# A scan pipeline in which the gated convolution starts two steps later on even steps, and 73 products change their engine

## The chip, the cores and the metric

The kernel runs on one core of a Trainium2 chip. Its time is the device time of one execution in microseconds (us); three executions before the change took 28298.65 us in the median (28296.38 to 28321.09). One further execution was recorded by the profiler; every duration below comes from that one.

## The reference

Two layers work on 8 images of 64 channels and 128 x 128 pixels, in float32. The first is a filter whose 3 x 3 weights are computed for each pixel (a convolution, a softmax over nine taps, a weighted sum of shifted pixels). The second is longer. Cut to what matters:

```
x_norm = ln4d(input)                       # layer norm over channels
seq = layernorm(x_norm as 16384 tokens)
for i in range(2):                         # two blocks, each scanned in both directions
    x, z = in_proj(rmsnorm(seq))
    yf = mamba_dir(x, z, forward);  yb = flip(mamba_dir(flip(x), flip(z), backward))
    seq = seq + out_proj(yf + yb)
x4 = conv3x3(rmsnorm(seq)) + residual
x = input + depthwise3x3(conv1x1(x_norm)) * x4
g1, g2 = split(depthwise3x3(conv1x1(ln4d(x))))      # 170 channels each
return x + conv1x1(gelu(g1) * g2)

# mamba_dir, for 128 channels d and 16 states n, along the tokens:
h = exp(softplus(dt) * A) * h + dt * B * u          # the recurrence
y = (sum over n of h * C + D * u) * silu(z)
```

The recurrence is the bulk: 8 images x 2 blocks x 2 directions x 128 channels x 16 states, each over 16384 tokens.

## The kernel before

**Chunks and steps.** A chunk is 1024 tokens of one image, block and direction. There are 512 of them, 64 to an image, and chunk i starts at step 16 i. A step `t` is one scan over 128 rows (32 channels times 4 states) of the chunk, so there are 8192 steps, 1024 to an image; `u` is the number of the step in its chunk, 0 to 15. "Step 9 of a chunk" below means u = 9. The chunk's work is in `Chunk.plan`:

- `drive` (L1236): GpSimd multiplies dt*u by B for two scans at once, 128 x 2048, into `bu` (4 buffers), on odd steps, five steps ahead of its first scan.
- `decay` (L1244): ScalarE's exponential for one scan, into one of two PSUM buffers `w`, two steps ahead.
- `scan` (L1263 one way, L1265 the other): VectorE's recurrence over 1024 tokens. It writes back to `w`, or to `hs` in SBUF where the product will be made on GpSimd.
- `product` (L1280 on VectorE, L1282 and L1284 on GpSimd): h times C. `on_pool(u)` chooses: odd u and u = 4, 12 go to VectorE in the same step, the other even u to GpSimd a step later, six in a chunk. An even step that follows a gelu (`gelu_times`) has its product on VectorE too.
- `keep` (L1287): ScalarE copies the last column as the next chunk's state. A column and the two buffers `w` tie ScalarE's exponentials to the product of two steps before.
- `collect` (L1295, L1302): TensorE sums the states of a pair of scans into `y`, at steps 4, 5, 7, 9, 12, 13, 15 and 17 of the chunk. `y` is one PSUM buffer, two halves of the chunk take it in turn; `y_out` empties it at steps 11 and 3 (L1317 on VectorE in a direction's second pass, where it also applies the gate; L1319 on ScalarE in the first pass).

The inputs of chunk i + 2 are made beside it, through one PSUM buffer `mm`: `xp` (L1111) is issued at steps 6 and 7, the gate's `zp` (L1126) at 8 and 9, `dp` (L1153) at 13 and 14, `bcp` (L1172) at 15. ScalarE empties each a step later (L1117, L1134, L1160, L1179), applies silu at step 11 (L1137, L1139) and softplus at step 2 (L1166), each between two loads of an activation table. The output projection `op` (L1331, L1334) is issued at step 4, also through `mm`, and emptied by L1337 and L1344 at step 6.

**Three more stages run beside the scans**, each over 16 row groups of an image: the front (filter and first norms of the next image, from step 593 of an image, 24 steps a group), the mix (both 3 x 3 convolutions, the product, a norm, from step 990, 13 steps a group, so it ends in the next image's step 200), and the FFN (the gated convolution of the image before, from step 1202, that is step 178 of the next image, 24 steps a group). So in images 1 to 6 the mix lies beside steps 990 to about 180, the FFN beside 178 to about 562, the front beside 569 to about 993. The last image has no front beside it: its steps from about 562 to 826 have the scans alone, and its mix starts at 826.

The FFN of a group at step a: windows are loaded; three groups of `conv` (L932, L938) are issued in four parts each, at a to a+3, a+6 to a+9 and a+14 to a+17; they write the PSUM buffers `acc` and `bg`. ScalarE copies the first group's result (`first_out`, L980, a+5) and applies `gelus` (L987, L989, a+11, between two table loads). VectorE multiplies: `rest_times` (L994) at a+13, `times` (L997) for half 0 at a+19 and half 1 at a+21. `project` (L1012 to L1018) follows at a+21, ScalarE empties it (`add`, L1024) at a+23. 24 is one and a half chunks, so two successive groups begin at u = 2 and u = 10; 48 steps, two groups and three chunks make one period.

The front's softmax for a group: less_max and exps on VectorE and ScalarE, `sums` on VectorE (L588), `softmax` on GpSimd (L592), then three `piece` copies on ScalarE (L596) with two `less_piece` subtractions on GpSimd (L600) between them, then `turn` on TensorE (L605) and `turned` on ScalarE (L609).

**Order.** Nothing is scheduled by a tool. Every piece is put under a key (step, phase) and the program is issued in the order of the keys; inside a step the phases are FEED, SCAN, MID, PROD, EXP, DECAY, REST. An engine works its instructions strictly in that order, so a late one holds up all that stand behind it. SyncE issues the loads and stores, in the same order.

Of the kernel before, what the change touches and what calls it, by code (L numbers as in the profile page):

```python
# [21 lines left out]
NCH = HALF // ROWS  # L22
# [9 lines left out]
NT = 2 * NCH * N // T  # L32
# [4 lines left out]
FEED, SCAN, MID, PROD, EXP, DECAY, REST = range(7)  # L37

IMAGE = 4 * NT * U
FRONT_STEP, MIX_STEP, FFN_STEP = 24, 13, 24  # L40
FRONT_AT, MIX_AT, FFN_AT = 593, 990, 1202

SILU, SOFTPLUS, GELU = 11, 18, 11

# [11 lines left out]
def kernel(ctx: ExitStack, tc: tile.TileContext, a: dict, out: bass.AP):  # L56
# [131 lines left out]
    with tc.tile_pool(name="wspill", bufs=1) as fp, tc.tile_pool(name="wprep", bufs=2) as pp, \  # L188
            tc.tile_pool(name="wps", bufs=4, space=PSUM) as pps:
        with tc.manual_schedule():  # L190
# [104 lines left out]
            for k in range(9):  # L295
                i, j = divmod(k, 3)
# [28 lines left out]
            for q, ((g, c0, r0, n), fn, fdn) in enumerate(parts):  # L325
# [7 lines left out]
                for k in range(9):  # L333
                    i, j = divmod(k, 3)
# [26 lines left out]
            for l in range(DEPTH):  # L361
# [3 lines left out]
                for d in range(2):  # L365
# [5 lines left out]
                    now, i = taps, 2 * l + d + 1  # L371
                    if i < 2 * DEPTH:
                        taps = by_taps(inx2[i // 2], dirs[i][0], DI, KC)
                    for j in range(KC):
                        t = turned(now[:, j, :], ident, P, DI)
                        at = j if d == 0 else KC - 1 - j
# [40 lines left out]
    def at(time, phase, fn, *args):  # L417
        steps.setdefault((time, phase), []).append((fn, args))
# [123 lines left out]
    class Front:  # L542
        def __init__(self, b, c):
            self.b, self.c, self.p = b, c, b % 2
            self.n1, self.n2, self.n3 = Norm(), Norm(), Norm()
            self.t, self.wbk, self.alone = {}, {}, False
# [149 lines left out]
        def plan(self, a):  # L696
            n1, n2, n3 = self.n1, self.n2, self.n3
            b = a - FRONT_STEP
            at(b - 5, REST, self.load_xa)
            for i in range(3):  # L700
                at(b + 1 + i, REST, self.hidden, i)
            at(b + 5, DECAY, self.hidden_out)
            at(b + 21, REST, self.logits)
            at(b + 23, DECAY, self.less_max)
            at(b + 23, DECAY, self.exps)
            at(b + 25, MID, self.sums)
            at(b + 25, REST, self.softmax)
            for i in range(3):
                at(b + 26 + 2 * i, DECAY, self.piece, i)
                if i < 2:  # L710
                    at(b + 27 + 2 * i, REST, self.less_piece, i)
            at(b + 31, REST, self.turn)
            at(b + 32, DECAY, self.turned)
            at(a + 6, REST, self.load_xb)
            for k in range(9):

                t = a + k
                at(t + 11, DECAY, self.weight, k)
                at(t + 12, MID, self.weighted, k)
                at(t + 13, REST, self.gather, k)  # L720
            at(a + 23, DECAY, self.filtered)
            at(a + 23, REST, self.store_x1)
            at(a + 23, REST, self.centered, acc_tile, "x1")
            at(a + 24, DECAY, self.centered_out)
            at(a + 25, REST, lambda: n1.means(bg_tile, self.sq))
            at(a + 26, DECAY, n1.means_out)
            at(a + 27, REST, n1.spread, bg_tile)
            at(a + 29, MID, self.scaled, n1)
            at(a + 29, DECAY, self.first_norm)
            at(a + 30, REST, self.pointwise)  # L730
            at(a + 31, DECAY, self.pointwise_out)
            at(a + 31, REST, self.store_rows, dw_img[self.p], "dwt")
            at(a + 31, REST, self.centered, acc_tile, "xn")
            at(a + 32, DECAY, self.centered_out)
            at(a + 33, REST, lambda: n2.means(acc_tile, self.sq))
            at(a + 34, DECAY, n2.means_out)
            at(a + 35, REST, n2.spread, acc_tile)
            at(a + 37, MID, self.scaled, n2)
            at(a + 37, DECAY, self.second_norm)
            at(a + 37, REST, self.store_h)  # L740
            late, end = (a + 46, a + 55) if self.c < NCH - 1 else (a + 37, a + 43)
            at(late, DECAY, self.third_square)
            at(late + 1, REST, lambda: n3.means(bg_tile, self.sq))
            at(late + 2, DECAY, n3.means_out)
            at(end - 2, REST, n3.spread, bg_tile)
            at(end, MID, self.third_norm)
            at(end, REST, self.store_hn)
# [145 lines left out]
    class Ffn:  # L893
# [139 lines left out]
        def plan(self, a):  # L1033
            early = 12 if self.alone else 0
            at(a - 4 - early, REST, self.load, 0)
            at(a - 3 - early, REST, self.load, 1)

            if self.alone:
                at(a - 6, REST, self.before_taps)
                at(a - 5, DECAY, self.before_taps_out)  # L1040
                at(a - 5, REST, self.taps, 0)
                at(a - 2, REST, self.taps, 1)
                groups = ((0, 0, self.first_out, 2), (3, 1, self.times, 6))
                gelus, out = 3, 9
            else:
                groups = ((0, 0, self.first_out, 5), (6, 2, None, 0), (14, 1, self.times, 19))
                gelus, out = GELU, 21
            for t, g, end, to in groups:
                for i in range(4):
                    at(a + t + (0 if self.alone else i), REST, self.conv, g, i)  # L1050
                for h in range(2 if end else 0):
                    late = 0 if self.alone or end == self.first_out else 2 * h
                    at(a + to + late, MID if end == self.times else DECAY, end, h)
            at(a + gelus, REST, self.gelus)
            at(a + gelus + 2, MID, self.rest_times)
            at(a + out - 5, REST, self.load_x2)
            at(a + out, REST, self.project)
            at(a + out + 2, DECAY, self.add)
            at(a + out + 2, REST, self.store)
# [18 lines left out]
    class Chunk:  # L1078


        def __init__(self, i):
            self.b, self.l, self.d, self.t, self.second = order[i]
            self.i, self.t0 = i, U * i
            self.first = i % NT == 0
            self.pairs = PAIRS[i % 2]
            r, last = self.t0 % IMAGE, self.b == B - 1
            self.beside_front = (
                FRONT_AT - FRONT_STEP <= r < FRONT_AT + NCH * FRONT_STEP + 16 and not last
            ) or self.t0 < FIRST_FRONT_AT + (NCH - ALONE) * FRONT_STEP + 16
            self.prev = None  # L1090
            self.bus, self.hss, self.hs, self.ws = {}, {}, {}, {}
            self.dup, self.dtp, self.bp, self.cp, self.yv = {}, {}, {}, {}, {}
            self.norm = Norm()
# [128 lines left out]
        def on_pool(self, u):  # L1222


            if u % 2 or u % 8 == 4 or self.t0 + u - 1 in gelu_times:
                return False
            return True

# [221 lines left out]
    for b in range(B):  # L1450
        a, last = IMAGE * b, b == B - 1
# [36 lines left out]
```

## Time and profile before

| | us |
|---|---|
| median of three executions | 28298.65 |
| profiled execution | 28309.23 |
| its span, first to last instruction | 28307.4 |
| VectorE (DVE) busy | 26958.6 (95%) |
| GpSimd (POOL) busy | 26592.1 (94%) |
| TensorE (PE) busy | 23060.5 (81%) |
| ScalarE (ACT) busy | 18801.5 (66%) |
| one scan, L1263 or L1265 | 2.34 |
| one product on VectorE, L1280 | 1.22 |
| one product on GpSimd, L1282 / L1284 | 2.37 / 2.38 |
| one drive on GpSimd, L1236 | 4.55 |
| one decay on ScalarE, L1244 | 1.12 |

The page shows VectorE at "6999...97" tenths and GpSimd at "5999...94" over 40 slices: both are busy nearly always, in every slice but the first and the last. There are 5232 products on VectorE and 2960 on GpSimd, 8192 together. A busy share is an average over stages with different limits, so the useful views are the same ones over one stage: the busy times of a stretch (the windows view), who waited for whom in it (the waits view, which gives total, times and longest), and the instructions in order of time (the timeline).

### The profile page before, as it was taken

What the parts mean: (1) busy time and instruction counts of PE and PEld (TensorE: products, weight loads), DVE (VectorE), ACT (ScalarE), POOL (GpSimd) and SP (SyncE); (2) the same over time, 40 slices, a digit from 0 to 9 for tenths busy, and PEclk for the clock granted to TensorE, in tenths of its full rate; (3) what the DMA queues carried; (4) which work ended last, traced back from release to release, by engine and by line L of the source; (5) the groups of instructions that cost most, each with busy time, mean ns of one, the idle gap of its engine ahead of it and who ended that gap; (6) DMA issues with size and microseconds to landing.
All of it is one profiled execution on the core that took longest, in us unless ns stands there. A gap on an engine that the chain in (4) does not pass through costs nothing. (4 is left out here: it accounts for less than half of the span.)

```text
span 28307.4 us, 311814 instructions
## 1 busy us (share of the span) xinstructions
PE 23060.5 (81%) x98278; PEld 7346.2 (26%) x98278; DVE 26958.6 (95%) x17398; ACT 18801.5 (66%) x29144; POOL 26592.1 (94%) x7980
## 2 busy tenths in 40 slices
PE   8667888878888788888888888787888978888679
PEld 3212322223222232222322222222222222222113
DVE  6999999999999999999999999999999999999997
ACT  4666666666666666666666666666666666666663
POOL 5999999999999999999999999999999999999994
PEclk8778889988999889988889888998888988889789
DMA  6777787767877778777787777777777777777675
GB/s 178 233 239 229 238 262 247 249 227 239 267 243 248 230 240 266 247 242 231 246 257 249 242 232 246 259 249 237 233 253 251 252 234 238 251 251 249 217 251 153
DMA packets 2611073, 6796.34 MB, mean 240 GB/s; under 512 B 433558, under 2 KB 739110, under 8 KB 2608390
## 3 DMA queue, kind: packets, MB, share of 16 engines
q1 hardware_dynamic: 2608534, 6776.25, 73.7%
q8 instruction: 776, 12.71, 0.2%
q14 instruction: 883, 7.23, 0.1%
q10 hardware_dynamic: 880, 0.14, 0.0%
HBM read 5543.05 MB, written 1265.19 MB: 241 GB/s over the span
## 5 line engine op out<-in xcount | busy, mean ns | idle before, releaser
L1236 POOL TENSOR_TENSOR bu<-dup,bp 128x2048 f32<-128x2048 f32 x4096 | 18600.2, 4549 | 59.5 <-DMA bp<-bc_dram 23.8
L1244 ACT ACTIVATE w<-dtp,a_neg 128x1024 f32<-128x1024 f32 x8192 | 9163.6, 1119 | 1444.9 <-DVE hs L1265 586.8
L1280 DVE TENSOR_TENSOR hs<-w,cp 128x1024 f32<-128x1024 f32 x5232 | 6390.3, 1221 | 191.1 <-DMA cp<-bc_dram 41.0
L1265 DVE TENSOR_TENSOR_SCAN w<-w,state,bu 128x1024 f32<-128x1024 f32 x2651 | 6210.2, 2343 | 90.7 <-ACT w L1244 60.3
L1263 DVE TENSOR_TENSOR_SCAN w<-w,state,bu 128x1024 f32<-128x1024 f32 x2581 | 6048.3, 2343 | 124.7 <-ACT w L1244 105.3
L1302 PE MATMUL y<-hs,sel_y 128*32 128x512 f32 x32768 | 4953.0, 682 | 580.9 <-POOL hs L1284 449.1
L1287 ACT COPY state<-w 128x1 f32<-128x1 f32 x5232 | 828.5, 158 | 5159.7 <-DVE hs L1280 5100.4
L1282 POOL TENSOR_TENSOR hs<-hs,cp 128x1024 f32<-128x1024 f32 x1515 | 3590.8, 2370 | 507.5 <-DVE hs L1263 316.3
L1284 POOL TENSOR_TENSOR hs<-hs,cp 128x1024 f32<-128x1024 f32 x1445 | 3432.9, 2376 | 394.0 <-DVE hs L1265 366.1
L1263 DVE TENSOR_TENSOR_SCAN hs<-w,state,bu 128x1024 f32<-128x1024 f32 x1515 | 3550.5, 2344 | 159.4 <-ACT state L1287 79.9
L1265 DVE TENSOR_TENSOR_SCAN hs<-w,state,bu 128x1024 f32<-128x1024 f32 x1445 | 3384.4, 2342 | 76.8 <-ACT state L1287 43.3
L1111 PE MATMUL xp<-hn,wx 128*128 128x512 f32 x4096 | 2502.6, 742 | 1171.9 <-ACT xc L1117 561.7
L932 PE MATMUL fp<-fw,bgw 128*128 128x512 f32 (+1 forms) x5760 | 2123.0, 614 | 37.8 <-DMA fw<-xn_dram 34.5
L1153 PE MATMUL dp<-xc,wdt 128*128 128x512 f32 x2048 | 1328.2, 735 | 690.6 <-ACT dt L1160 390.3
L1302 PEld LDWEIGHTS y<-hs,sel_y 128*32 128x32 f32 x32768 | 719.7, 114 | 4287.9 <-issue 2594.1
L1295 PE MATMUL y<-xc,dskip 128*64 128x512 f32 x4096 | 1371.0, 754 | 417.8 <-ACT yv L1319 315.5
L1111 PEld LDWEIGHTS xp<-hn,wx 128*128 128x128 f32 x4096 | 849.0, 225 | 2656.4 <-issue 1047.3
L68 ACT ACT_TABLE_LOAD x1137 | 1458.8, 1283 | 20.9 <-PEq L1477 0.7
L1117 ACT ACTIVATE xc<-xp,cbias 128x512 f32<-128x512 f32 x1024 | 701.7, 685 | 1151.4 <-PE xp L1111 1149.1
L938 PE MATMUL fp<-fw,bgw 64*128 64x512 f32 (+1 forms) x5760 | 1379.1, 605 | 0.0
L634 PE MATMUL acc<-t,ident 128*128 128x512 f32 x2250 | 1353.6, 690 | 0.0
L619 PE MATMUL wb<-wt,sel_k 65*128 65x512 bf16 x1152 | 509.4, 443 | 992.9 <-DVE t L623 988.5
(220 smaller groups left out, 26201.6 us busy)
## 6 DMA issues: line engine op xcount, KB each, us to landing
bp<-bc_dram SPq DMA_DIRECT2D x4096, 256.0 KB
dup<-du_dram SPq DMA_DIRECT2D x4096, 256.0 KB
dtp<-dt_dram SPq DMA_DIRECT2D x4096, 256.0 KB
cp<-bc_dram SPq DMA_DIRECT2D x4096, 256.0 KB
hn<-hn_dram SPq DMA_DIRECT2D x1024, 256.5 KB
dt_dram<-dt SPq DMA_DIRECT2D x512, 512.0 KB
du_dram<-du SPq DMA_DIRECT2D x512, 512.0 KB
yf_dram<-yv SPq DMA_DIRECT2D x512, 256.0 KB
```

Source lines behind the costliest of these rows:

```text
L68: nc.scalar.preload_act_table_set("natural_log_exp_and_others")
L932: nc.tensor.matmul(o, wpair[:, i, g, m], self.win[h][:, i : i + ROWS, 0:W], start=(i == 0), stop=False)
L938: nc.tensor.matmul(o, wlast[rows, i, g, m], self.win[h][rows, i : i + ROWS, lo : W + lo], start=False, stop=(i == 2),)
L1111: nc.tensor.matmul(self.xp[h], wx[:, self.l, self.d, i, :], self.hn2[:, s.start + 2 * i : s.stop + 2 * i], start=(i == 0), stop=(i == 1),)
L1236: nc.gpsimd.tensor_tensor(bu, self.dup[self.pairs[k][1]], self.over_pair("bp", k), ALU.mult)
L1244: nc.scalar.activation(w, self.dtp[gp][:, i, :], AF.Exp, scale=a_neg[:, self.l, self.d, g, j : j + 1])
L1263: nc.vector.tensor_tensor_scan(to, w, bu, s0, ALU.mult, ALU.add)
L1265: nc.vector.tensor_tensor_scan(to[:, ::-1], w[:, ::-1], bu[:, ::-1], s0, ALU.mult, ALU.add)
L1280: nc.vector.tensor_tensor(out, hs, c, ALU.mult)
L1282: nc.gpsimd.tensor_tensor(out, hs, c, ALU.mult)
L1284: nc.gpsimd.tensor_tensor(out[:, ::-1], hs[:, ::-1], c[:, ::-1], ALU.mult)
L1302: nc.tensor.matmul(self.y[lo : lo + 32, :], sel_y, hs[:, i, s], start=False, stop=(k % 4 == 3))
```

## The change

The FFN starts at step 1204 in place of 1202, and its VectorE products move to even steps: `rest_times` from a+13 to a+14, both `times` to a+20 (from a+19 and a+21). `project` moves from a+21 to a+20, `load_x2` and `add` with it. As the gelus stand at a+11, the even step whose product goes to VectorE because of them moves from u = 14 and 6 to u = 0 and 8. The front's `softmax`, its pieces, `turn` and `turned` move one step back. Last, in every second chunk that has neither front nor FFN beside it, from chunk 16 on, the product of u = 8 goes to VectorE.

```diff
-FRONT_AT, MIX_AT, FFN_AT = 593, 990, 1202
+FRONT_AT, MIX_AT, FFN_AT = 593, 990, 1204
...
-            at(b + 25, REST, self.softmax)
+            at(b + 26, REST, self.softmax)
             for i in range(3):
-                at(b + 26 + 2 * i, DECAY, self.piece, i)
+                at(b + 27 + 2 * i, DECAY, self.piece, i)
                 if i < 2:
-                    at(b + 27 + 2 * i, REST, self.less_piece, i)
-            at(b + 31, REST, self.turn)
-            at(b + 32, DECAY, self.turned)
+                    at(b + 28 + 2 * i, REST, self.less_piece, i)
+            at(b + 32, REST, self.turn)
+            at(b + 33, DECAY, self.turned)
...
-                groups = ((0, 0, self.first_out, 5), (6, 2, None, 0), (14, 1, self.times, 19))
-                gelus, out = GELU, 21
+                groups = ((0, 0, self.first_out, 5), (6, 2, None, 0), (14, 1, self.times, 20))
+                gelus, out = GELU, 20
...
-                    late = 0 if self.alone or end == self.first_out else 2 * h
-                    at(a + to + late, MID if end == self.times else DECAY, end, h)
+                    at(a + to, MID if end == self.times else DECAY, end, h)
             at(a + gelus, REST, self.gelus)
-            at(a + gelus + 2, MID, self.rest_times)
+            at(a + gelus + (2 if self.alone else 3), MID, self.rest_times)
...
+            beside_ffn = FFN_AT - IMAGE <= r < FFN_AT - IMAGE + NCH * FFN_STEP and self.b
+            self.few_steps = self.i >= NT and not self.beside_front and not beside_ffn
...
             if u % 2 or u % 8 == 4 or self.t0 + u - 1 in gelu_times:
                 return False
+            if u == 8 and self.i % 2 and self.few_steps:
+                return False
             return True
```

Counted in the changed program, VectorE has 5305 products and GpSimd 2887: 73 have moved. By the conditions they lie in 10 chunks of image 0 (17 to 35), in 7 chunks of each of the seven mix stretches between images (49), in 7 chunks of the last image's scans alone, and in 7 beside its mix. The last image's own FFN, with nothing beside it, is as before.

## The prediction

> **What bounds the kernel now.** The page puts VectorE at 95% and GpSimd at 94%, and the chain of work that ended last is followed there through too small a share of the span to choose. I therefore read, stage by stage, first the busy times of one stretch, then who waited for whom in it, then the timeline. The four stretches are the scans beside the mix, beside the FFN, beside the front, and alone (last image). The columns are start and end, length, then busy time and instructions by engine, TensorE's granted clock, DMA share, GB/s.
>
> ```profile
> 7193.70:7879.80 686.10, 553.71 (x2446) 157.54 (x2444) 652.71 (x379) 455.33 (x692) 678.59 (x195) 0.90 0.83 264
> 7879.80:9100.80 1221.00, 1063.47 (x4346) 324.90 (x4350) 1182.83 (x712) 839.86 (x1235) 1162.07 (x330) 0.94 0.74 244
> 9254.80:10648.00 1393.20, 1152.00 (x5201) 405.95 (x5200) 1350.52 (x945) 954.91 (x1561) 1324.68 (x423) 0.87 0.73 237
> 26520.00:27039.00 519.00, 280.78 (x894) 52.63 (x896) 485.74 (x260) 317.56 (x454) 519.00 (x151) 0.62 0.60 205
> ```
>
> The order of engines is PE, PEld, DVE, ACT, POOL. Scans alone: GpSimd is busy 519.00 of 519.00 us. FFN and front: VectorE is the busier one (97%). Mix: GpSimd has 99%, VectorE 95%. Whether GpSimd sets the pace there is told by VectorE's waits. Scans alone (window 26520 to 27039):
>
> ```profile
> DVE hs L1265 <- POOL bu L1236: 18.6, 29, 1.0
> DVE w L1265 <- POOL bu L1236: 7.5, 8, 0.9
> ```
>
> VectorE waits here for GpSimd's drive about four times a chunk. Mix (7193.7 to 7879.8):
>
> ```profile
> DVE hc L654 <- PE rb L514: 10.8, 5, 3.8
> DVE w L1263 <- ACT w L1244: 7.7, 7, 2.3
> DVE hs L1263 <- ACT w L1244: 4.7, 3, 2.7
> ```
>
> These are its three longest; no row of this view names a drive. GpSimd is just full there, and VectorE waits for TensorE and ScalarE. Beside the FFN (7879.8 to 9100.8), the same three engines:
>
> ```profile
> DVE yv L1317 <- PE y L1302: 7.8, 8, 2.6
> DVE w L1265 <- ACT w L1244: 6.1, 6, 1.7
> DVE ga L997 <- PE fp L938: 3.8, 4, 1.0
> DVE w L1263 <- ACT w L1244: 3.0, 2, 2.5
> ```
>
> The timeline tells why, first TensorE, then VectorE, at the second group of a period (xp is issued at u = 6, the group's last convolutions at u = 8 to 11):
>
> ```profile
> 8276.04 3.54 PE L1111 MATMUL xp<-hn,wx 128*128 128x512 f32 x4 [3.73 <-ACT state L1287]
> 8280.59 1.98 PE L1111 MATMUL xp<-hn,wx 128*128 128x512 f32 x4
> 8284.35 1.99 PE L932 MATMUL fp<-fw,bgw 128*128 128x512 f32 x4
> ```
>
> ```profile
> 8284.53 2.36 DVE L1265 TENSOR_TENSOR_SCAN w<-w,state,bu 128x1024 f32<-128x1024 f32 x1 [0.78 <-ACT w L1244]
> 8287.40 0.69 DVE L1317 TENSOR_TENSOR yv<-y,gate 128x512 f32<-128x512 f32 x1 [0.52 <-DMA o<-branch_dram]
> 8295.96 0.69 DVE L997 TENSOR_TENSOR ga<-ga,fp 128x512 f32<-128x512 f32 x1 [0.95 <-PE fp L938]
> ```
>
> TensorE idles 3.73 us before xp, then needs 3.54 us for four matmuls that take 1.98 us a little later. ScalarE's copy of xp is late, its exponentials behind it are late, and the convolutions stand in front of the collect that y_out needs.
>
> **The change, part by part.** All sums are against the profiled execution, 28309.2 us, which is 10.6 us above the median of the runs.
>
> *Prices.* Around 8220 us a step with its product on VectorE takes 3.51 us (scan starts 8223.74 and 8227.25), one without 2.25 us (8221.49 to 8223.74). So a moved product costs VectorE 1.26 us; it saves GpSimd 2.37 less the 0.05 us by which its instructions overlap, 2.32 us. A step with product and one of the FFN's multiplications between takes 3.96 us (8217.53 to 8221.49), so that multiplication costs 0.45 us, because the product had to wait for the scan anyway. On an even step nothing has to wait, and it costs its own 0.67 us less the 0.08 us overlap, 0.59 us.
>
> *FFN, seven images of 16 groups.* Removed: in steps 8 to 11 there are no convolutions ahead of the collect any more (a group's parts now stand at u = 4 to 7, 10 to 13 or 2 to 5); the parts at 2 to 5 fill TensorE's idle time before xp; times comes three steps after its last convolution instead of two. I strike the four rows above, 7.8 + 6.1 + 3.8 + 3.0 = 20.7 us an image, and leave the rows of the silu, which stays. Added: 3 x 16 multiplications x 0.14 us = 6.7 us, since VectorE is the bound. Added too: the gelus hold ScalarE for 4.3 us (two table loads of 1.28 us, with activations of 0.60, 0.62 and 0.62 us between them that overlap a little; 8189.3 to 8193.5 us in the trace). After them the next decay needs 1.3 us (0.16 for the kept column, 1.12 for itself). With 1.9 us in front (the decay ahead, 1.12, and a copy, 0.69) that is 7.5 us against the two product steps, 7.0 us, that VectorE has; rest_times, which gave 0.45 us more cover at a+13, is now a step later. So 0.4 us at each of 16 groups, or nothing if the copies are early: 0 to 6.4, I take 3.2 us. Last, at the group that now starts at u = 4, TensorE has op, three collects, xp and 8.8 us of convolutions in about 19 us; queued behind are zp and the collect for y_out, and behind ScalarE's copy of zp the decays. Counting the queue I find the collect 0 to 1.1 us late; nearest is the same group at u = 2 now, where y_out follows without a wait, so 0.5 us, 4.0 us an image. Net 20.7 - 6.7 - 3.2 - 4.0 = 6.8 us an image, **48 us** in seven; with both bounds from 98 us gained to 8 us lost. SyncE's FFN loads move with the group and none of these rows waits for a window.
>
> *Products beside the mix, 49.* VectorE pays 8.8 us in a stretch (7 x 1.26). A part is absorbed: the product at u = 8 gives ScalarE and TensorE 1.26 us more before the waits at u = 10 and 11, which I find in four of the seven chunks (2.2, 1.0, 0.9 and 0.8 us), so about 4 us. GpSimd's gain helps only where TensorE waited for a GpSimd product, 11.8 us in four waits of this stretch; one of them, 4.6 us, precedes a wait of VectorE of 2.7 us. Net 8.8 - 4 - 2.7 - 2 = **0 us**, bounds 8.8 us lost to 8 us gained a stretch, that is 61 lost to 56 gained in all.
>
> The Trainium skill, Perfetto Trace Analysis, section Identifying the Most-Contended Engine, says that the most occupied engine is the bottleneck and to be relieved first. That is GpSimd in the mix stretch, 678.6 against 652.7 us, and by that rule 7 x 2.32 = 16 us a stretch would be gained, 114 us in all. The waits view speaks against it, and I go by the waits.
>
> *Products in the scans alone, 7.* GpSimd sets the pace, so each saves up to 2.32 us: 16 us, less the first, where drives are still ahead: **15 us** gained. *Image 0, 10:* GpSimd is full in its second half too, but y_out and norms bring VectorE within 1 us of it a chunk, so about half, **12 us** gained. *Beside the last mix, 7:* as in the mix, with little to absorb, **5 us** lost.
>
> *Front.* The softmax product (0.31 us) no longer stands ahead of GpSimd's product, and the first piece (0.24 us) leaves the front of the silu, behind whose end the scan at u = 14 waits. Six such chunks an image, 1.4 us; six images and a little: **8 us** gained. GpSimd is not the bound there, so its own waits pay nothing. What is late next is turned, still two steps ahead of its first use.
>
> Sum: 48 + 0 + 15 + 12 - 5 + 8 = 78 us less. 28309 - 78 = 28231 in the profiled execution, **28220 us** as a median.
>
> **Rivals.**
>
> *The waits move and nothing is gained.* The new waits behind gelus and first group stand at their upper ends (FFN 8 us lost) and the small terms stay (30 gained): about 28280 us. For it speaks that both ends were counted from full queues; against it, that TensorE loses its cold xp.
>
> *Larger gain.* No new wait in the FFN (98), the mix gains 56, the rest 30: 28115 us. For it, GpSimd's 99%; against it, no wait for a drive in 686 us.
>
> *Slower: TensorE's queue at u = 4 to 9.* If the group that now starts at u = 4 runs on the slow matmuls (3.54 in place of 1.98 us), its 8.8 us become nearly twice that, and zp, the collect and ScalarE's decays are some 4 us late in every period, 56 periods. That costs 224 us, plus 47 for the even steps, less 145 struck and 30 elsewhere: 96 us lost, 28395 us. It decides from 2.3 us of new waits a period; TensorE's idle time in front of xp there, now under 2 us by my count, speaks against it.
>
> **How the numbers follow.** Likeliest 0.50, at 28220 us (its own range 28170 to 28260); moved waits 0.23; larger gain 0.15; slower 0.12. The range 28110 to 28310 us holds the first three but for edges and leaves the slower case out. About 0.2%, 57 us, is what a measurement of this kernel can tell from no change: below 28242 lie the larger gain and five sixths of the likeliest, 0.57; within 0.2%, the rest of it and the moved waits, 0.31; above 28355, 0.12.
>
> **What would show it.** Beside the FFN, the rows yv and ga fall to under 2 us an image and xp never takes 3.5 us for four matmuls; new rows of w behind ScalarE at u = 2 and 10 of 0.4 us; a step with two times on it takes 3.4 us. The mix stretches keep 686 us within 5, with GpSimd below 97%. The scans alone lose about 1 us a chunk, and VectorE's waits for bu fall there. I am wrong if the mix stretches change by more than 8 us, or if collects at u = 9 hold y_out by over 1 us.

## The result, and the profile after

The changed kernel takes 28523.17 us in the median of four executions (28514.64 to 28527.01); the kernel before took 28301.43 us in the four beside it. The ratio is 1.0078 (95% interval 1.0065 to 1.0091): some 222 us slower, where 78 us less was forecast. Its profiled execution took 28527.01 us with a span of 28525.2 us, so the two traces differ by 217.8 us. The starts of the scans divide that difference by stage:

| stage | before, us | after, us | difference | forecast |
|---|---|---|---|---|
| beside the FFN, seven images, 23 chunks each | 8544.3 | 8809.1 | +264.8 | -48 |
| three chunks behind it, six images | 922.1 | 940.5 | +18.4 | with the front |
| beside the front, six images, 25 chunks each | 8364.8 | 8330.7 | -34.1 | -8 |
| beside the mix, seven times 13 chunks | 4795.0 | 4790.1 | -4.9 | 0 |
| image 0, chunks 13 to 34 | 1141.1 | 1124.8 | -16.3 | -12 |
| last image, scans alone, 16 chunks | 827.1 | 812.9 | -14.2 | -15 |
| last image, beside its mix, 12 chunks | 640.7 | 642.8 | +2.1 | +5 |

Outside the FFN and the three chunks behind it, the stages came out near the forecast in size or at least in sign. The page alone would not have told this. These are its engine totals for the changed kernel; VectorE has the 95% it had before, over a longer span:

```profile
PE 23308.5 (82%) x98278; PEld 7428.0 (26%) x98278; DVE 27083.3 (95%) x17471; ACT 18815.4 (66%) x29144; POOL 26424.2 (93%) x7907
```

The busy times of the four stretches that the prediction read, now for the changed kernel (start and end, length, then PE, PEld, DVE, ACT, POOL, the granted clock, DMA share, GB/s; the last stretch is 510 us of the scans alone):

```profile
7213.60:7898.10 684.50, 555.35 (x2456) 155.80 (x2454) 658.83 (x383) 451.68 (x686) 659.33 (x188) 0.90 0.83 264
7898.10:9157.50 1259.40, 1091.83 (x4344) 336.40 (x4340) 1190.05 (x711) 845.26 (x1240) 1165.94 (x331) 0.92 0.74 238
9314.60:10702.50 1387.90, 1158.87 (x5201) 405.67 (x5194) 1350.01 (x946) 955.25 (x1562) 1317.52 (x421) 0.87 0.72 236
26750.00:27260.00 510.00, 277.17 (x904) 51.88 (x896) 493.67 (x268) 319.02 (x459) 510.00 (x146) 0.66 0.62 211
```

In the mix GpSimd is down from 678.6 to 659.3 us, and the length from 686.1 to 684.5 us only: it was full there, but not in the way. In the scans alone it is still busy for every microsecond, and there each product taken from it paid. Beside the FFN the stretch is 38.4 us longer, of which VectorE's own work is 7.2 us (1190.05 less 1182.83). The rest is waiting. VectorE's waits there (engine, line, what it waited for: us in total, times, longest):

```profile
DVE hs L1268 <- ACT w L1247: 32.0, 13, 3.3
DVE w L1268 <- ACT w L1247: 13.2, 14, 2.0
DVE hs L1268 <- ACT state L1290: 6.5, 14, 0.5
DVE w L1266 <- ACT w L1247: 3.5, 3, 2.4
```

(Line numbers are three higher than before, those of xp and dp one.) The rows of yv and ga, 7.8 and 3.8 us before, are gone, as forecast. The two rows of w that the prediction also struck, 6.1 and 3.0 us before, are not: they stand at 13.2 and 3.5 us. And there is a new first row: 32.0 us in 13 waits for a decay, in front of scans whose product is GpSimd's (they write hs). The timeline shows one of them, the longest, first ScalarE, then VectorE, then TensorE:

```profile
8472.68 0.69 ACT L1118 ACTIVATE xc<-xp,cbias 128x512 f32<-128x512 f32 x1 [2.62 <-PE xp L1112]
8473.39 1.28 ACT L987 ACT_TABLE_LOAD   x1
8474.68 0.60 ACT L987 ACTIVATE gt<-fp 128x512 f32<-128x512 f32 x1
8475.17 1.14 ACT L989 ACTIVATE ga<-ga 128x512 f32<-128x512 f32 x2
8476.33 1.28 ACT L68 ACT_TABLE_LOAD   x1
8477.62 0.16 ACT L1290 COPY state<-w 128x1 f32<-128x1 f32 x1
8477.82 1.12 ACT L1247 ACTIVATE w<-dtp,a_neg 128x1024 f32<-128x1024 f32 x1
```

```profile
8474.50 1.23 DVE L1283 TENSOR_TENSOR hs<-w,cp 128x1024 f32<-128x1024 f32 x1
8479.02 2.35 DVE L1268 TENSOR_TENSOR_SCAN hs<-w,state,bu 128x1024 f32<-128x1024 f32 x1 [3.30 <-ACT w L1247]
```

```profile
8466.22 3.65 PE L938 MATMUL fp<-fw,bgw 64*64 64x512 f32 x16
8469.80 1.12 PE L1315 MATMUL y<-yf,ident 128*128 128x512 f32 x2
8470.76 1.88 PE L1112 MATMUL xp<-hn,wx 128*128 128x512 f32 x4
```

Read it from the end. The scan of step 10 starts 3.30 us late because its decay (8477.82) is. The decay stands behind the gelus, which take 4.2 us from 8473.39, and the gelus of step 7 stand behind the copy of xp, for which ScalarE idled 2.62 us: TensorE had the last convolutions, 3.65 us, and the sum of yf, 1.12 us, before xp. Nothing in this chain is slow; each piece is only behind the other. Half a period, 24 steps, later the same happens at step 15 with the copy of dp, which waits 2.10 us; there the scan of step 2 is 2.69 us late (ScalarE, then VectorE):

```profile
8556.76 0.69 ACT L1161 ACTIVATE dt<-dp,dtb 128x512 f32<-128x512 f32 x1 [2.10 <-PE dp L1154]
8563.10 2.35 DVE L1268 TENSOR_TENSOR_SCAN hs<-w,state,bu 128x1024 f32<-128x1024 f32 x1 [2.69 <-ACT w L1247]
```

ScalarE's own waits tell how much of this is new. Two rows of an image, first before, then after:

```profile
ACT xc L1117 <- PE xp L1111: 50.3, 33, 2.7
...
ACT dt L1160 <- PE dp L1153: 1.7, 2, 1.0
```

```profile
ACT xc L1118 <- PE xp L1112: 55.1, 30, 4.2
...
ACT dt L1161 <- PE dp L1154: 25.0, 29, 2.1
```

The copy of dp waits only since the change. That of xp waited nearly as much before, and cost VectorE little. What is new at step 7 is what stands behind it.

Averaged over 35 periods of 48 steps (the third to seventh of each image, counted here from step 192 of the image, so that step 0 of a period is u = 0), a period went from 160.56 to 166.64 us. The scan after step 1 is 2.78 us later, the one after step 25 (u = 9) 3.21 us, the one after step 42 (u = 10) 1.75 us; the multiplications on even steps cost 0.8 us net, the moved gelu products 0.1 us, and the rest, taken as what remains of the difference and chiefly the waits that went, is 2.6 us less.

### The profile page after: what moved, and what is told of

Read it like the earlier page. It is cut to its first block, busy times and chain, and to the rows that moved or that the text cites. A ratio compares the mean times of both kernels' runs of the same rounds, so it can differ in the third digit from the quotient of the medians.

```text
span 28525.2 us, 311825 instructions
## 1 busy us (share of the span) xinstructions
PE 23308.5 (82%) x98278; PEld 7428.0 (26%) x98278; DVE 27083.3 (95%) x17471; ACT 18815.4 (66%) x29144; POOL 26424.2 (93%) x7907
## 5 line engine op out<-in xcount | busy, mean ns | idle before, releaser
L1283 DVE TENSOR_TENSOR hs<-w,cp 128x1024 f32<-128x1024 f32 x5305 | 6483.9, 1222 | 195.4 <-DMA cp<-bc_dram 24.2
L1268 DVE TENSOR_TENSOR_SCAN w<-w,state,bu 128x1024 f32<-128x1024 f32 x2667 | 6252.1, 2344 | 147.0 <-ACT w L1247 135.6
L1266 DVE TENSOR_TENSOR_SCAN w<-w,state,bu 128x1024 f32<-128x1024 f32 x2638 | 6183.3, 2344 | 82.6 <-ACT w L1247 79.6
L1305 PE MATMUL y<-hs,sel_y 128*32 128x512 f32 x32768 | 5026.5, 686 | 328.3 <-POOL hs L1287 264.6
L1285 POOL TENSOR_TENSOR hs<-hs,cp 128x1024 f32<-128x1024 f32 x1458 | 3443.7, 2362 | 694.9 <-DVE hs L1266 442.7
L1287 POOL TENSOR_TENSOR hs<-hs,cp 128x1024 f32<-128x1024 f32 x1429 | 3378.3, 2364 | 661.5 <-DVE hs L1268 420.7
L1268 DVE TENSOR_TENSOR_SCAN hs<-w,state,bu 128x1024 f32<-128x1024 f32 x1429 | 3347.6, 2343 | 293.6 <-ACT w L1247 233.4
L1266 DVE TENSOR_TENSOR_SCAN hs<-w,state,bu 128x1024 f32<-128x1024 f32 x1458 | 3417.3, 2344 | 158.3 <-ACT w L1247 98.4
L1112 PE MATMUL xp<-hn,wx 128*128 128x512 f32 x4096 | 2406.9, 718 | 888.9 <-ACT xc L1118 391.3
L932 PE MATMUL fp<-fw,bgw 128*128 128x512 f32 (+1 forms) x5760 | 2391.6, 658 | 199.7 <-DVE gt L994 172.2
L68 ACT ACT_TABLE_LOAD x1137 | 1458.8, 1283 | 20.7 <-PEq L1480 0.7
```

Source lines behind the costliest of these rows:

```text
L68: nc.scalar.preload_act_table_set("natural_log_exp_and_others")
L932: nc.tensor.matmul(o, wpair[:, i, g, m], self.win[h][:, i : i + ROWS, 0:W], start=(i == 0), stop=False)
L1112: nc.tensor.matmul(self.xp[h], wx[:, self.l, self.d, i, :], self.hn2[:, s.start + 2 * i : s.stop + 2 * i], start=(i == 0), stop=(i == 1),)
L1266: nc.vector.tensor_tensor_scan(to, w, bu, s0, ALU.mult, ALU.add)
L1268: nc.vector.tensor_tensor_scan(to[:, ::-1], w[:, ::-1], bu[:, ::-1], s0, ALU.mult, ALU.add)
L1283: nc.vector.tensor_tensor(out, hs, c, ALU.mult)
```

## The experiments

In the runs of the experiments the kernel before took 28320 to 28332 us, some 20 to 30 us more than above; experiment 8 shows where. Each kernel is therefore compared with the runs of before beside it.

| run | us | before beside it, us | ratio (95% interval) |
|---|---|---|---|
| 1, FFN part alone | 28571.66 | 28331.74 | 1.0084 (1.0069 to 1.0099) |
| 2, all but the FFN part | 28315.98 | 28331.74 | 0.9994 (0.9985 to 1.0003) |
| 3, FFN's start alone | 28637.61 | 28331.74 | 1.0108 (1.0093 to 1.0123) |
| 4, even steps alone | 28369.28 | 28331.74 | 1.0012 (1.0002 to 1.0022) |
| 5, gelus ahead of the copies | 28395.50 | 28329.55 | 1.0024 (1.0014 to 1.0033) |
| 6, no table loads | 28310.59 | 28329.55 | 0.9992 (0.9983 to 1.0002) |
| 7, short second convolution | 28403.24 | 28329.55 | 1.0025 (1.0015 to 1.0035) |
| 8, before, traced again | 28325.22 | 28329.55 | single run |
| 9, the parts that gained | 28279.95 | 28319.71 | 0.9985 (0.9976 to 0.9994) |
| 10, both times together | 28272.23 | 28319.71 | 0.9984 (0.9975 to 0.9993) |

**Which part.** The four first kernels divide the change.

Experiment 1 has only the FFN's part:

```diff
+FRONT_AT, MIX_AT, FFN_AT = 593, 990, 1204
...
+                groups = ((0, 0, self.first_out, 5), (6, 2, None, 0), (14, 1, self.times, 20))
+                gelus, out = GELU, 20
...
+            at(a + gelus + (2 if self.alone else 3), MID, self.rest_times)
```

> Only the FFN's part of the change: its start two steps later and its VectorE products on even steps; softmax and products beside the other stages as before. If the loss lies wholly in the FFN's stretches (the stage times of the two traces give +260 us there and +20 us in the three chunks behind each, -62 us elsewhere), about 28301 + 280 = 28580 us. If the loss needs the other parts too (products or softmax pushing work into the FFN's stretch), clearly less, under 28500 us.

It is 240 us slower than before; the FFN stretches take 8801.3 us in its trace (8809.1 in the changed kernel, 8544.3 before). The FFN's part carries the whole loss and needs no other part for it.

Experiment 2 is the reverse, the front's softmax a step later and `few_steps`, with the FFN of before.

> The change without its FFN part: softmax a step later and five products on GpSimd in every second chunk beside neither front nor FFN. If the parts add up, 28301 - 62 = about 28240 us, with image 0 about 16 us, the last image's scans alone about 14 us and the six fronts together about 30 us shorter. If the shorter fronts came from the FFN's shift, only the first two terms remain, about 28270 us.

It gained 16 us of the 62, with an interval that takes in no change. Image 0, the scans alone and the fronts came out as expected (1125.2, 812.1 and 8330.9 us in its trace), so the fronts do not owe their gain to the FFN. The expectation failed in two places. Beside the mixes its trace is longer, 4810.2 us in seven stretches and 647.0 in the last image, against 4796.8 and 641.8 in experiment 8, a later trace of the kernel before. And it lost just before the fronts: the chunk at step 592 takes 55.0 to 55.4 us, against 51.1 us without the shift. There GpSimd's softmax, one step later, stands behind a drive, and ScalarE's piece waits for it with the decays behind it (ScalarE in experiment 2's trace):

```profile
16134.92 0.25 ACT L596 CAST sp<-lg 128x72 bf16<-128x72 f32 x1 [3.86 <-POOL lg L592]
16135.08 0.15 ACT L1291 COPY state<-w 128x1 f32<-128x1 f32 x1
16135.26 2.15 ACT L1248 ACTIVATE w<-dtp,a_neg 128x1024 f32<-128x1024 f32 x2
16141.98 0.25 ACT L596 CAST sp<-lg 128x72 bf16<-128x72 f32 x1 [4.56 <-POOL lg L600]
```

So the shift of softmax pays 34 us in the fronts and gives about 25 us back (six times 4.2) at their first row group.

Experiments 3 and 4 divide the FFN's part. Experiment 3 has `FFN_AT` = 1204 and all distances as before; experiment 4 has `FFN_AT` = 1202 and the products on even steps.

> The FFN starts at 1204, but its products keep their old distances from the start (rest_times at +13, times at +19 and +21, projection at +21), and softmax and the other products stay. Theory: the start is the cause; the gelus now stand at steps 7 and 15, behind ScalarE's copies of the first xp and the second dp, which wait for convolutions two steps later in TensorE's queue, and the decay behind them is late by 2 to 3 us twice in 48 steps. Then 28500 to 28600 us, with VectorE's waits for w at steps 2 and 10. Rival: the even steps are the cause (three multiplications a group that nothing covers, and the rest's cover a step later); then here only small terms, 28280 to 28340 us.

> The FFN starts at 1202 as before, but its products stand on even steps (rest_times at +14, times and projection at +20). Theory (the start is the cause): 3 x 16 x 0.14 us an image dearer, 47 us in all, less up to 27 us where the wait of ga for its convolution goes: 28290 to 28350 us. Rival (the even steps are the cause): 28450 us or more, with waits for w after the gelus at steps 0 and 8.

The start alone costs 306 us, more than the whole part: steps 1 and 25 take 6.30 and 6.66 us (6.29 and 6.91 in the changed kernel, 3.51 and 3.70 before), and `times` on its odd steps waits for its convolution besides (VectorE in experiment 3, second image):

```profile
DVE ga L997 <- PE fp L938: 25.9, 9, 5.3
DVE hs L1265 <- ACT w L1244: 18.5, 10, 1.9
```

The row of ga was 3.8 us before, and I had not expected it to grow: the time is 38 us above the top of what I had put down. The even steps alone cost 38 us against the 28331.74 beside them, within the 20 to 47 us worked out. That the sum fits is in part luck: in the trace steps 10 and 11 of a period take 8.62 us together in the mean, 6.99 before, because the projection, now a step earlier, stands in TensorE's queue ahead of the second half of xp (read from the timeline), and no such term had been put down. Start and even steps together cost less than the sum of both because the even steps take the waits for the convolution away (no row of ga is left in experiment 1). The start is the cause; that it is the even steps is refuted.

**Why the start.** In the changed kernel the gelus stand at steps 7 and 15 (before at 5 and 13), and the convolutions of a group stand two steps nearer to the next projection. Three edits of the changed kernel take one link each out of the chain.

Experiment 5 issues the gelus ahead of the copy in their step:

```diff
-            at(a + gelus, REST, self.gelus)
+            at(a + gelus, REST if self.alone else EXP, self.gelus)
```

> The changed kernel with one edit: in the gelus' step they are issued ahead of ScalarE's copies (of the first xp at step 7, of the second dp at step 15) and not behind them. Theory: the loss is the gelus' 4.3 us standing behind a copy that waits 2.1 to 2.6 us for TensorE; then VectorE's stalls before the scans at steps 2 and 10 (2.8 and 3.4 us a period of 48 steps) fall to about 0.6 us each, some 5 us in each of about 50 periods, 200 to 250 us less than the changed kernel, of which up to 100 us may come back where the copies, and with them the next projections, are later (the stall at step 11, now 1.7 us a period): 28350 to 28450 us where the kernel before takes 28330. Rival (TensorE is simply late there, and whoever waits for it first pays): within 50 us of the changed kernel, about 28550 us.

It is 66 us slower than before, not 222: 156 us of the loss are gone by a change of order alone, with the same work on every engine. VectorE's waits in the second image show which (the first row of the changed kernel was 32.0 us in 13 waits):

```profile
DVE w L1268 <- ACT w L1247: 11.4, 16, 2.0
DVE hs L1268 <- ACT state L1290: 7.1, 14, 0.9
DVE hs L1268 <- ACT w L1247: 6.8, 13, 0.6
```

The same 13 waits are there, and none is over 0.6 us, as worked out. The period is 160.93 us, within 0.4 us of before. What is left of the loss lies mostly at the two ends of the FFN: the first two periods and the last are together some 13 us an image dearer, about 95 us in seven images, against which stands what the other parts of the change gain.

Experiment 6 leaves gelu out (identity in its place), and with it the two table loads:

```diff
-                nc.scalar.activation(self.gt, self.rest[0], AF.Gelu)
+                nc.scalar.activation(self.gt, self.rest[0], AF.Identity)
...
-            if not self.alone:
-                logs_and_exps()
```

> The changed kernel with the identity in place of gelu beside the scans, so that the two table loads of each gelu group fall away and its hold of ScalarE shrinks from 4.3 to about 1.8 us; it leaves gelu out. Theory: the stalls at steps 2 and 10 shrink by 2.5 us each, 5 us in each of about 50 periods, 250 us in all: about 28300 us where the kernel before takes 28330. Rival (TensorE's queue delays xp, dp and everything behind them, whatever the gelus take): less than 80 us gained, above 28470 us.

The loss is gone, 19 us less than before with an interval that takes in no change (the parts outside the FFN gave 16 us in experiment 2): the same order and the same late xp (ScalarE waits 2.62 us for it in the same chunk), only a shorter hold. Steps 1 and 25 take 3.52 and 3.94 us where the changed kernel takes 6.29 and 6.91. At these two steps a late xp or dp costs VectorE little as long as nothing long stands behind its copy.

Experiment 7 keeps gelus and order and cuts the second convolution group to its first tap (the others are left out):

```diff
+            if g == 2 and not self.alone and part:
+                return
```

> The changed kernel with the second group of each convolution cut to the first of its taps (the other taps are left out), so that most of the convolutions that stand right ahead of the projections xp and dp at steps 2 to 5 and 10 to 13 are gone, and the gelus stand where the change put them. Theory in its full form (a copy late behind these convolutions, gelus behind the copy): the stalls at steps 2 and 10 fall from 2.8 and 3.4 us to under 0.8 us, 28250 to 28330 us where the kernel before takes 28330. If the place of the gelus behind a copy is enough without late convolutions, the stalls stay over 1.5 us each and the time stays above 28400 us.

It is neither: 74 us slower than before. At step 15 the theory held (step 1 takes 4.11 us, a stall of 0.6 us); at step 7 half of the stall stayed (5.37 us, 1.86 us over 3.51). Its trace tells why, first TensorE, then ScalarE:

```profile
8440.52 3.78 PE L1114 MATMUL xp<-hn,wx 128*128 128x512 f32 x4 [5.55 <-ACT sq L1349]
8444.23 1.94 PE L1307 MATMUL y<-hs,sel_y 128*32 128x512 f32 x8
8446.10 2.05 PE L1114 MATMUL xp<-hn,wx 128*128 128x512 f32 x4
```

```profile
8443.10 0.17 ACT L1292 COPY state<-hs 128x1 f32<-128x1 f32 x1
8444.34 0.69 ACT L1120 ACTIVATE xc<-xp,cbias 128x512 f32<-128x512 f32 x1 [1.06 <-PE xp L1114]
8445.05 1.28 ACT L989 ACT_TABLE_LOAD   x1
```

Without the convolutions TensorE idles 5.55 us in front of xp and then works at half speed, 3.78 us for four matmuls that take 2.05 us later (the granted clock is 0.50 in the first of the two, 1.00 in the second). The copy still waits, 1.06 us in place of 2.62. So the late convolutions are the cause at step 15. At step 7 they are one of two ways in which xp is late (its copy waited 50.3 us an image before the change already), and the gelus' new place behind that copy is the fault.

**The control.** Experiment 8 is the kernel before, traced once more.

> The kernel before, unchanged, for a trace of it beside the others of this set: three kernels of the first set took 57 to 58 us for the chunk at step 560 of an image, where the two traces shown first took 52 to 54 us, with waits for the load of cp. If that comes from the chip or the run and not from the edits, this trace has about 57 us there too and is about 30 us longer than 28309 us; if it comes from the edits, it repeats 52 to 54 us.

It has 56.6 to 58.0 us in that chunk in all six images, where the first trace of it has 52.6 to 54.3. VectorE's wait for cp in one of them, first in the first trace of before, then here:

```profile
DVE hs L1280 <- DMA cp<-bc_dram: 4.0, 2, 3.1
```

```profile
DVE hs L1280 <- DMA cp<-bc_dram: 9.3, 2, 5.5
```

The program is the same, so this term belongs to the chip or the run, which were not told apart, and not to an edit. Some 4 us in six images are 25 us, more than the 16 us by which the two traced executions differ (28309.23 and 28325.22 us).

**A kernel out of what gained.** Experiment 9 is the kernel before with five products on GpSimd in image 0 and in the last image's scans alone, not beside a mix, and softmax a step later for all row groups but the first; experiment 10 puts both `times` of a group at a+21 besides.

```diff
+            late = b + (self.c > 0)
+            at(late + 25, REST, self.softmax)
...
+            self.few_steps = self.i >= NT and not self.beside_front and not beside_ffn and not self.beside_mix
```

> The kernel before with those parts of the change alone that gained in the stage times: five products on GpSimd in every second chunk of image 0 (without its last, beside the mix) and of the last image's scans alone, not beside any mix, and softmax a step later for all row groups of the front but the first (where the trace shows GpSimd behind a drive and ScalarE's pieces late, 4 us a front). Sum of stage times: -16 (image 0), -15 (scans alone), -34 (six fronts), 0 for the rest: about 65 us below the kernel before, 28265 us where that takes 28330. If the gain of the fronts is only moved in time, about 28300 us.

> The same, and in the FFN at its old start both times of a group stand at +21 (before: +19 and +21). The wait of the first for its convolution (0.9 us at step 13 of one chunk in three, about 45 us in all) goes, and the second multiplication on one step costs 0.67 in place of 0.45 us, 112 x 0.22 = 25 us: about 20 us below the kernel without it, 28245 us where the kernel before takes 28330; if the two multiplications and the product make the step too long for ScalarE's next decays or for the collect, 28290 us or more.

Both beat the kernel before, by 40 and 47 us (intervals 0.9976 to 0.9994 and 0.9975 to 0.9993), and the changed kernel, measured by its own runs of before, by more than 250 us. Experiment 9 missed 25 of the 65 us: against experiment 8, image 0 gave 18 us and the scans alone 16 us, the fronts only 15 us of 34. The chunk at step 592 is back at 51.1 us, but the next takes about 55 us where the full shift has 53 to 54, six times some 2 us; that part of the fronts' gain had only been moved. The two `times` together are 8 us faster, not the 20 us expected, and these intervals do not tell 8 us from nothing.

## Why the prediction was wrong

Its terms, per period of 48 steps beside the FFN, with the share of each in the forecast (an image's figure over eight periods) and what the traces gave:

| step of the prediction | forecast, us | measured, us |
|---|---|---|
| four rows of waits that go | -2.6 | -2.6 (remainder) |
| three multiplications a group on even steps | +0.8 | +0.8 |
| decay behind the gelus, two groups | +0.4 | +6.0 |
| TensorE's queue at the group that starts at u = 4 | +0.5 | +1.75 |

**The step that failed** is the one on the gelus: "With 1.9 us in front ... that is 7.5 us against the two product steps, 7.0 us". Place and mechanism were right; it asked for waits of 0.4 us behind ScalarE at steps 2 and 10, and there they are, seven times as large. The term in front was mis-sized: its wait was put at nothing. I counted the copy by its own 0.69 us, as if its data were there. It stands in ScalarE's queue ahead of the gelus and waits for TensorE, 2.10 us for dp and 2.62 us for xp; 7.5 + 2.1 and 7.5 + 2.6 less 7.0 are 2.6 and 3.1 us, against 2.78 and 3.21 measured (the terms of the 7.5 add up to 7.39; it is that sum that gave 0.4). Experiments 5 and 6 show this by taking away the order or the length of the hold. For xp the row that would have warned was in the profile of before: ScalarE waited 50.3 us an image for it, in 33 waits of up to 2.7 us. VectorE felt little of it then because the gelus were not behind that copy. For dp no row warned (1.7 us in 2 waits): that wait came with the change, from the convolutions that now stand ahead of dp. The prediction had counted the convolutions at u = 2 to 5 as gain alone. They do keep xp fast at step 7, 1.88 us for four matmuls, but xp starts behind them and its copy still waits 2.62 us. The bound that I gave the term, 0 to 6.4 us an image, was worked out from durations alone and could not hold a wait.

**The second term**, TensorE's queue, was mis-sized by a factor of three. In one of three chunks xp still comes after an idle time (2.66 us) on slow matmuls, 3.68 us for four, then convolutions stand between its halves, ScalarE waits 3.99 us for the second and the scan of step 11 is 2.00 us late (TensorE, ScalarE, VectorE in the changed kernel):

```profile
8524.57 3.68 PE L1112 MATMUL xp<-hn,wx 128*128 128x512 f32 x4 [2.66 <-ACT sq L1347]
8533.98 0.69 ACT L1118 ACTIVATE xc<-xp,cbias 128x512 f32<-128x512 f32 x1 [3.99 <-PE xp L1112]
8535.90 2.36 DVE L1268 TENSOR_TENSOR_SCAN w<-w,state,bu 128x1024 f32<-128x1024 f32 x1 [2.00 <-ACT w L1247]
```

The sign "xp never takes 3.5 us for four matmuls" was wrong. This was the rival that ended on the slower side; it put 4 us a period on it, measured were 1.75, below the 2.3 us from which it was to decide. The kernel is slower all the same, by a mechanism that I had priced at a fifteenth. A further rival, gelus behind a waiting copy, was missing, and the two signs of being wrong that the prediction named did not give it away: no mix stretch changed by more than 8 us, and VectorE's waits for y_out's collect beside the FFN, 6.3 to 7.8 us an image before, are down to 0.3 us or none.

**What was right.** The multiplications, to about a tenth of a microsecond a period, and the sum of the waits that go, though not each row: those of yv and ga went, those of w did not. The mix: no wait for a drive there, and with 49 products off GpSimd the 7 stretches changed by -4.9 us; the rule weighed in the prediction would have given 114 us. The -4.9 is not the products' alone. The FFN's later start takes 1.4 us off the last chunk of each stretch (52.21 to 50.77 us), 10 us in all, and experiment 2, with the FFN of before, is 13 us longer in these stretches than experiment 8. Single stretches differ by up to 4 us between the two traces of the kernel before, so the products may have cost a few us there; none of it is near a gain of 114. The forecast of 0 also leaned on a deduction of 2 us a stretch for which the prediction names no source. Scans alone and image 0: -14.2 and -16.3 us against 15 and 12. A step with two `times` takes 3.43 us. The fronts gained four times what I had put down (34 against 8); with the 25 us lost at their first row group, which I had not seen, the net is about the 8. Both sizes were off, and the sum is right by chance.

One figure bears on the length of the gelus' hold, and the trace decides against half of it. The Trainium skill, ScalarE: Activation LUTs, section What ACT_TABLE_LOAD costs, gives a switch of tables 1283 ns for the load and about 1380 ns for a drain. The rows above have 1.28 us for the load, and the next activation starts 0.01 us behind its end (8473.39 + 1.28, then 8474.68): no drain is seen. By the page's figures, as an estimate, the two switches would hold ScalarE for 5.3 us; the two loads in the trace take 2.6.

What stays open: why the two ends of the FFN stay dearer in experiment 5 was not followed up, and the 1.75 us at step 10 was not isolated by a kernel of its own. In experiments 5, 6 and 7 it is 0.94, 1.23 and 1.44 us, so none of these edits takes it away; that slow matmuls and the convolutions between xp's halves make it is read from the timeline only.

## What to carry to other kernels

ScalarE worked its queue in order here: the gelus stood ready behind a copy that waited 2.62 us. So a long piece of work that is moved must be costed with what stands right ahead of it in the queue and with that one's wait, not with its duration; look in the waits view for the engine that the piece runs on, not only for the engine that sets the end. A wait that costs nothing now (here ScalarE's for xp) becomes the price of whatever long thing is put behind it. And when two deadlines meet in one step, try the order inside the step first: here one changed phase gave back 156 of 222 us.

## What the runs showed of the hardware

TensorE's half speed followed both a 5.55 us and a 2.66 us idle time: four matmuls of xp took 3.78 and 3.68 us, against 1.98 us at full clock. In the second case the granted clock is 1.00 up to 8524.5 us and 0.50 from 8526 to 8528. Taking work away from TensorE (experiment 7) brought the slow matmuls back where the convolutions had kept the clock at 1.00. The Trainium skill, TensorE: Matmul & The Clock Gate, Part 1, puts the fall to half the clock behind an idle window of about 3.4 us; the row with 2.66 us is shorter than that.

One and the same program waited 4.0 us for the loads of cp in a chunk of one run and 9.3 us in another, and between these sets of runs its median moved by about 0.1%: as much as some of the terms that were to be told apart here.
